# Reordering the first products of two accumulation stages in a cross-attention and expert kernel

## The chip, the cores and the metric

The kernel runs on one core of one Trainium2 chip. The metric is device microseconds of one execution; several executions are timed and their median is given. A separate profiled execution gives the trace, with its own time beside its span (from the first to the last instruction).

The engines are named as the profile names them: PE is the matrix engine and PEld its weight loads, DVE the vector engine, ACT the engine for activation functions, POOL the general one, SP the one whose queue issues most of the transfers. PE writes its products to banks of the accumulation memory (PSUM); the kernel uses eight banks of 128 x 512 fp32.

## What is computed

One transformer layer over 2048 tokens of width 256, in fp32: causal self attention, cross attention to 1601 context rows, a feed-forward block, and a layer of eight experts of which each token uses two.

```
def layer(y, Z):                       # y: layernorm of x, 4 blocks of 512 tokens here
    sa = attention(y, y, y, causal=True)
    y  = layernorm(y + sa, g1, beta1)
    ca = attention(y, Z, Z, causal=False)
    y  = layernorm(y + ca, g2, beta2)
    ff = relu(y @ w1 + b1) @ w2 + b2
    return layernorm(y + ff, g3, beta3)
x = x + layer(layernorm(x), ctx)
h = layernorm(x)
x = x + sum over the top 2 of 8 experts: weight * ((silu(h @ w1e) * (h @ w3e)) @ w2e)
```

In both attentions a score matrix is exponentiated without a division. The values carry a column of ones as a 257th column, so that one product gives the weighted sum and the sum of the weights together, and the division is made afterwards on 128 rows at a time.

## The kernel before

The 2048 tokens are four blocks (`b` = 0 to 3) of four tiles of 128 tokens (`j` = 0 to 3). The stages follow one another on PE: self attention of blocks 0, 1 and 2, the cross scores of block 0 (`cross_scores(0)`), self attention of block 3, and then for each block `cross_values(b)`, `cross_scores(b + 1)` and `ffn(b)`; last come the expert tiles. PE's order is the order in which the program is written (`manual_schedule` for the tensor engine, line 634). The other engines are put in order by a planner from the dependencies, except where the program says `issue_after`.

Eight banks are in three pools: `ps_s` with four (`bank_s`), `ps_o` with two (`bank_o`), `ps_t` with two. A pool hands out its banks in turn, and a bank is written again only when the last reader of its previous content is done. So the four accumulators of one stage take over the four `ps_s` banks that the stage before it used, in the same order.

Two stages matter here.

*Self attention of a block, `self_block` (lines 470 to 513).* `weigh` makes the scores of all 512 queries of the block against one tile of 128 keys in a `bank_o` (`scores`, line 380, products called `ss`), exponentiates them on ACT into a tile `pT` (line 363, four buffers), and masks the diagonal part on POOL (line 367). `values` (line 494, products called `acc`) multiplies the four query tiles with the values of these keys and adds into the four accumulators `acc[0..3]` of the block. The loop runs one step ahead: scores of step i + 1, then values of step i. The last step takes two key tiles together. When a query tile has seen its last key, `attended` (lines 388 to 393) empties its accumulator on DVE: a reciprocal (line 390), a scale and add to `h` (line 392, the last reader of the bank), and then the statistics and scaling of the layer norm (lines 227 to 250), with a power on POOL (line 233).

Block 0 has a routine of its own, `first_self`, which ends with `attended` for its four tiles. Block 1 is the first that goes through `self_block`; its four accumulators take the banks of block 0's.

*Cross values, `cross_values` (lines 599 to 628).* The exponentiated cross scores of a block lie in `raw`, 13 tiles of keys (12 of 128 and one of 65). For each tile of keys `k`, four products (line 604, called `co`), one per query tile `j`, add into the accumulators `co_0` to `co_3`. Then DVE empties these (lines 616 and 618), and the normalised rows are sent across partitions by transfers on SP's queue (`cross_over`, line 293, into `tb_y`) and turned by DVE (`turn_within`, line 305) into `yT`, which `ffn(b)` reads. These turns stand inside `cross_scores(b + 1)`, behind the maxima (line 561) of keys 6 and 8.

`cross_values(0)` stands right behind the self attention of block 3, so `co_0` to `co_3` take over the banks of that block's `acc_0` to `acc_3`. Between these two stages SP's queue also issues the crossing of block 3's rows (line 293), eight loads of expert weights `wo` (line 676) and two of `wi` (line 689, called at line 695).

Every fp32 product on PE is two records in the trace, so that the four products of one key tile are eight records.

Of the kernel before, what the change touches and what calls it, by code (L numbers as in the profile page):

```python
# [15 lines left out]
P = 128  # L16
# [3 lines left out]
def xattn_ffn_moe(  # L20
# [21 lines left out]
    nc = tc.nc  # L42

    S, D = x.shape
# [6 lines left out]
    TPB = TB // P  # L51
# [3 lines left out]
    NK = (SK + P - 1) // P  # L55
# [35 lines left out]
    def bank_s(name):  # L91
        return ps_s.tile([P, 512], F32, tag="s", name=name)

    def bank_o(name):
        return ps_o.tile([P, 512], F32, tag="o", name=name)
# [48 lines left out]
    z_sb = zpool.tile([P, NK, D + 1], F32, tag="z", name="z_sb")  # L144
# [94 lines left out]
    def normalize(dst, src, name, gain=None, shift=None, whole=None, behind=None):  # L239

        mean, rs = moments(src if whole is None else whole, name)
        if gain is None:
            return scaled(dst, src, mean, rs).ins
        n = work.tile([P, D], F32, tag="n", name=f"n_{name}")
        if len(dst.shape) > 2:
            n, gain, shift = qn(n), qn(gain), qn(shift)
            src = qn(src) if len(src.shape) == 2 else src
        nc.vector.scalar_tensor_tensor(n, src, mean, gain, ALU.subtract, ALU.mult)
        with tc.issue_after(behind) if behind is not None else ExitStack():
            return nc.vector.scalar_tensor_tensor(dst, n, rs, shift, ALU.mult, ALU.add).ins  # L250
# [22 lines left out]
    def quarters(b):  # L273


        together = ya[b].rearrange("p j n -> p (j n)")[:, : TPB * D]
        return together.rearrange("p (q j n) -> p q j n", q=NQ, j=TPB)

    def mid(t):
        return quarters(t // TPB)[:, :, t % TPB, :]  # L280

    def qn(a):
        return a.rearrange("p (q n) -> p q n", q=NQ)

    def crossing(name, b):
        return tbp.tile([P, TPB * D], F32, tag="tb", name=f"tb_{name}_{b}")

    def cross_over(tb, js, src):


        o, n = js[0], len(js)
        for q in range(NQ):
            last = nc.sync.dma_start(
                tb[q * Q : (q + 1) * Q, o * D : (o + n) * D], src[:, q, o : o + n, :]
            )
        return last.ins

    def turn_within(tb, into, js, behind=None, order="p i (c r) -> p i c r"):

        o, n = js[0], len(js)  # L300
        of = tb[:, o * D : (o + n) * D].rearrange("p (i j m) -> p i j m", i=NQ, j=n)
        for k, j in enumerate(js):
            to = into[:, :, j * P : (j + 1) * P]
            with tc.issue_after(behind) if behind is not None else ExitStack():
                done = nc.vector.transpose(
                    to.rearrange("p c (t i) -> p i c t", i=NQ),
                    of[:, :, k, :].rearrange(order, r=Q),
                )
        return done.ins
# [11 lines left out]
    for t in range(NT):  # L321
# [3 lines left out]
        else:  # L325
            b, j = divmod(t, TPB)
# [33 lines left out]
    def attend(pt, s):  # L360


        nc.scalar.activation(pt, s, AF.Exp, scale=SCALE)  # L363

    def mask(pt):

        nc.gpsimd.affine_select(
            pt,
            pt,
            pattern=[[1, P]],  # L370
            compare_op=ALU.is_ge,
            fill=0.0,
            base=0,
            channel_multiplier=-1,
        )

    def scores(s, b, kt, j0, j1):

        for c in range(ND):
            nc.tensor.matmul(  # L380
                s,
                lhsT=y0T[kt // TPB][:, c, (kt % TPB) * P : (kt % TPB + 1) * P],
                rhs=y0T[b][:, c, j0 * P : j1 * P],
                start=(c == 0),
                stop=(c == ND - 1),
            )

    def attended(acc, t):
        r = small.tile([P, 1], F32, tag="r", name=f"r1_{t}")
        nc.vector.reciprocal(r, acc[:, D : D + 1])  # L390
        h = work.tile([P, D], F32, tag="h", name=f"h1_{t}")
        nc.vector.scalar_tensor_tensor(h, acc[:, :D], r, y0[t][:, :D], ALU.mult, ALU.add)  # L392
        normalize(mid(t), h, f"1_{t}", g1b, be1b)
# [76 lines left out]
    def self_block(b, ptp, hooks):  # L470
        acc = [bank_s(f"acc_{b}_{j}") for j in range(TPB)]
        last = (b + 1) * TPB - 1

        def weigh(kts):

            s = bank_o(f"ss_{b}_{kts[0]}")
            pt = ptp.tile([P, TB], F32, tag="pt", name=f"pT_{b}_{kts[0]}")
            at, of = 0, []
            for kt in kts:

                j0 = max(0, kt - b * TPB)
                n = TB - j0 * P
                scores(s[:, at : at + n], b, kt, j0, TPB)
                of.append((kt, pt[:, at : at + n], j0))
                at += n
            attend(pt[:, :at], s[:, :at])
            for kt, p, _ in of:
                if kt >= b * TPB:
                    mask(p[:, :P])
            return of  # L490

        def values(kt, pt, j0):
            for j in range(j0, TPB):
                nc.tensor.matmul(  # L494
                    acc[j][:, : D + 1],
                    lhsT=pt[:, (j - j0) * P : (j - j0 + 1) * P],
                    rhs=y0[kt],
                    start=(kt == 0),
                    stop=(kt == b * TPB + j),
                )  # L500
            if kt >= b * TPB:
                attended(acc[j0], b * TPB + j0)


        steps = [[kt] for kt in range(last - 1)] + [[last - 1, last]]
        p = weigh(steps[0])
        for i in range(len(steps)):
            nxt = weigh(steps[i + 1]) if i + 1 < len(steps) else None
            for of in p:
                values(*of)  # L510
                if of[0] in hooks:
                    hooks[of[0]]()
            p = nxt
# [23 lines left out]
    raw = cp.tile([P, NK, TB], F32, tag="raw", name="raw")  # L537
# [5 lines left out]
    def keys(k):  # L543
        return P if k < KFULL else KREST
# [53 lines left out]

    def cross_values(b, js, hooks):
        acc = {j: bank_s(f"co_{b}_{j}") for j in js}  # L600
        for k in range(NK):
            n = keys(k)
            for j in js:
                nc.tensor.matmul(  # L604
                    acc[j][:, : D + 1],
                    lhsT=raw[:n, k, j * P : (j + 1) * P],
                    rhs=z_sb[:n, k, :],
                    start=(k == 0),
                    stop=(k == NK - 1),
                )  # L610
            if k in hooks:
                hooks[k]()
        for j in js:
            t = b * TPB + j
            r = small.tile([P, 1], F32, tag="r", name=f"r2_{t}")
            nc.vector.reciprocal(r, acc[j][:, D : D + 1])
            with tc.issue_after(turned_half[-1]) if turned_half else ExitStack():
                nc.vector.scalar_tensor_tensor(
                    mid(t), qn(acc[j][:, :D]), r, mid(t), ALU.mult, ALU.add
                )  # L620
        for j in js:
            t = b * TPB + j
            normed2.append(normalize(mid(t), mid(t), f"2_{t}", g2b, be2b))
        if b not in crossed:
            crossed[b] = crossing("y2", b)
        for h in range(0, len(js), 2):
            if b < LAST or js[0] == 0:
                cross_over(crossed[b], js[h : h + 2], quarters(b))


    ALL = range(TPB)
# [8 lines left out]
    for b in range(NB):  # L640
# [7 lines left out]
        hooks = {}  # L648
# [460 lines left out]
    def place_at(b):  # L1109
        puts = routed[b]()  # L1110
        if b == NB - 1:
            return puts
        for put in puts:
            put()
        if b == NB - 3:
            tabs["ex0"], tabs["row0"], tabs["done"] = tables_0()
        if b == NB - 2:
            tabs["exa"], tabs["rowa"], tabs["done"] = tables_a(tabs["done"])

    for b in range(NB - 1):  # L1120

        cross_values(b, ALL, {10: lambda: route_at(b - 1)} if b > 0 else {4: lambda: turn_y1(LAST)})
        hooks = {3: lambda: place_at(b - 1)} if b > 0 else {}
        cross_scores(b + 1, hooks, {6: ALL[:2], 8: ALL[2:]})
        ffn(b, ALL, {1: lambda: largest(b + 1), 3: lambda: exponentials(b + 1)})

    b, H = NB - 1, TPB // 2
    cross_values(b, ALL[:H], {})
    cross_values(b, ALL[H:], {NK - 1: lambda: turned_half.append(turn_within(crossed[b], yT[b], ALL[:H]))})
    load_xf(b)  # L1130
    route_at(b - 1)
# [153 lines left out]
    def turn_tile(n):  # L1285
        if n < len(tiles):
            xT[n] = turn_in(tiles[n][0], xs.pop(n))
# [11 lines left out]
    with tc.manual_schedule(engines={nc.sync.engine}):  # L1299
# [9 lines left out]
    hooks = {  # L1309
        2: lambda: turn_within(crossed[b], yT[b], ALL[H:]),  # L1310
        4: lambda: place_at(b - 1),
        NF - 1: lambda: [turn_tile(n) for n in range(2)],
    }
# [144 lines left out]
```

## Time and profile before

| what | us |
|---|---|
| three timed executions | 639.84, 642.43, 643.62 (median 642.43) |
| the profiled execution: its own time | 642.52 |
| the profiled execution: its span | 640.70 |
| PE busy in the span | 623.8 (97%) |
| PEld busy | 408.8 (64%) |
| DVE busy | 332.4 (52%) |
| POOL busy | 169.8 (26%) |
| ACT busy | 141.7 (22%) |

The stages of the profiled execution, by the start times of PE's instructions from the start of the span:

| stage | from, us | to, us |
|---|---|---|
| self attention of block 0 | 1.5 | 17.2 |
| self attention of blocks 1 and 2 | 17.2 | 77.6 |
| cross scores of block 0 | 77.6 | 99.9 |
| self attention of block 3 | 99.9 | 150.5 |
| cross values of block 0 | 150.5 | 174.7 |
| cross scores of block 1 | 174.7 | 197.0 |
| feed-forward of block 0 | 197.0 | 224.5 |
| blocks 1 and 2 in the same way | 224.5 | 373.8 |
| cross values and feed-forward of block 3 | 373.8 | 426.4 |
| expert tiles | 426.4 | 632.5 |
| last scatter and end | 632.5 | 640.7 |

A line of the timeline gives a start, a length, an engine and line, the operation with its output and inputs, and how many records were merged into it. In square brackets stands the idle time of the engine ahead of it and what ended it. The length of a matmul record reaches over the start of the next one, because products overlap in the array; the distance from one start to the next is the pace.

### The profile page before, as it was taken

The page shows a single profiled execution, that of the slowest core. Times are in us where ns is not written, and L with a number is a line of the kernel's source. Part 1 is how long each engine was busy: PE and PEld are TensorE (multiplying, and loading weights), DVE is VectorE, ACT ScalarE, POOL GpSimd, SP SyncE. Part 2 cuts the span into 40 slices and gives each one's busy share as a digit, 9 for nine tenths or more (in the row PEclk, how much of TensorE's full clock was granted, in tenths as well). Part 3 has the DMA queues.
Part 4 walks back from the last instruction along what each step waited for, and adds up shares of the span by engine and source line. Part 5 has one row for each costly group of instructions (what it writes and reads, how often), then busy time and mean ns, then how long its engine had stood idle before and what let it go on. Part 6 is the DMA issues. An engine that isn't in the chain of part 4 may idle for free. (4 is left out here: it accounts for less than half of the span.)

```text
span 640.7 us, 8263 instructions
## 1 busy us (share of the span) xinstructions
PE 623.8 (97%) x2255; PEld 408.8 (64%) x2256; DVE 332.4 (52%) x1011; ACT 141.7 (22%) x251; POOL 169.8 (26%) x240
## 2 busy tenths in 40 slices
PE   9999999999999999999999999999999999999993
PEld 8576745667845687467854688876665555555552
DVE  6662363504274476763587567737743344434341
ACT  3111132123033501352033600334211111111110
POOL 6221100002050032701155022443363222222222
PEclk9999999999999999999999999999999999999998
DMA  8999997001930012200312004953455555555532
GB/s 213 265 250 291 323 246 205 1 0 58 330 105 4 0 28 76 79 20 1 92 37 72 2 13 142 330 153 63 58 103 115 103 97 95 100 105 98 94 76 31
DMA packets 105549, 71.63 MB, mean 112 GB/s; under 512 B 43357, under 2 KB 99870, under 8 KB 105502
## 3 DMA queue, kind: packets, MB, share of 16 engines
q1 hardware_dynamic: 82510, 54.65, 31.9%
q0 software_dynamic: 6864, 9.08, 8.5%
q10 hardware_dynamic: 16128, 7.35, 4.0%
q8 instruction: 20, 0.33, 0.2%
q14 instruction: 27, 0.22, 0.1%
HBM read 28.11 MB, written 29.30 MB: 90 GB/s over the span
## 5 line engine op out<-in xcount | busy, mean ns | idle before, releaser
L233 POOL TENSOR_TENSOR rs<-ve,neghalf 128x1 f32<-128x1 f32 x80 | 47.6, 602 | 214.6 <-DVE ve L231 212.0
L604 PE MATMUL co<-z_sb,raw 128*128 128x257 f32 (+1 forms) x416 | 91.9, 381 | 1.1 <-DVE r L390 1.0
L551 PE MATMUL cs<-yT,zT_sb 128*128 128x512 f32 (+1 forms) x208 | 90.4, 593 | 0.0
L604 PEld LDWEIGHTS co<-z_sb,raw 128*128 128x128 f32 (+1 forms) x416 | 78.6, 190 | 13.0 <-issue 1.9
L551 PEld LDWEIGHTS cs<-yT,zT_sb 128*128 128x128 f32 (+1 forms) x208 | 38.5, 186 | 47.7 <-issue 46.1
L1207 PE MATMUL h_a<-wi,xT_a 128*128 x136 | 62.5, 594 | 0.0
L743 PE MATMUL fo<-w_sb,fhs 128*128 128x256 f32 x256 | 61.1, 380 | 0.0
L494 PE MATMUL acc<-y,pT 128*128 128x257 f32 x252 | 60.2, 381 | 0.8 <-DVE h L392 0.5
L721 PE MATMUL fh<-yT,w_sb 128*128 128x512 f32 (+1 forms) x160 | 60.9, 508 | 0.0
L494 PEld LDWEIGHTS acc<-y,pT 128*128 128x128 f32 x252 | 47.4, 190 | 18.8 <-issue 12.4
L743 PEld LDWEIGHTS fo<-w_sb,fhs 128*128 128x128 f32 x256 | 48.3, 190 | 16.0 <-issue 8.6
L558 ACT COPY raw<-cs 128x512 f32<-128x512 f32 (+1 forms) x52 | 30.4, 585 | 92.9 <-PE cs L551 92.9
L380 PE MATMUL ss<-y0T,y0T 128*128 128x512 f32 x96 | 44.6, 592 | 0.0
L1207 PE MATMUL h_b<-wi,xT_b 128*128 x96 | 43.3, 592 | 0.0
L730 ACT ACTIVATE fhs<-fh,b_sb 128x512 f32<-128x512 f32 (+1 forms) x40 | 24.0, 600 | 81.8 <-PE fh L721 81.8
L721 PEld LDWEIGHTS fh<-yT,w_sb 128*128 128x128 f32 x160 | 30.0, 190 | 17.2 <-issue 13.1
L1258 POOL DMA_INDIRECT out_dram<-yw_a,at_a x17 | 26.6, 1565 | 52.9 <-DVE yw_a L1256 29.4
L363 ACT ACTIVATE pT<-ss 128x512 f32<-128x512 f32 (+3 forms) x37 | 20.8, 562 | 86.8 <-PE ss L380 84.0
L561 DVE TENSOR_TENSOR top<-cs,top 128x512 f32<-128x512 f32 (+1 forms) x44 | 30.2, 687 | 16.9 <-ACT raw L558 16.0
L1207 PEld LDWEIGHTS h_a<-wi,xT_a 128*128 128x128 f32 x136 | 25.1, 190 | 21.8 <-issue 21.0
L1248 PE MATMUL y_a<-wo,gT_a 128*128 x136 | 32.4, 381 | 1.5 <-DVE gT_a L1231 1.5
L1248 PEld LDWEIGHTS y_a<-wo,gT_a 128*128 128x128 f32 x136 | 25.1, 190 | 13.6 <-DVE gT_a L1231 7.1
(267 smaller groups left out, 748.7 us busy)
## 6 DMA issues: line engine op xcount, KB each, us to landing
slots<-empty SPq DMA_DIRECT2D x8, 2064.0 KB
wo<-in_m2T_dram SPq DMA_DIRECT2D x8, 512.0 KB
wi<-in_m1T_dram SPq DMA_DIRECT2D x4, 1024.0 KB
wi<-in_m3T_dram SPq DMA_DIRECT2D x4, 1024.0 KB
gb_b<-g_b ACTq DMA_DIRECT2D x44, 64.0 KB
gb_a<-g_a ACTq DMA_DIRECT2D x36, 64.0 KB
xs_a<-slots SPq DMA_DIRECT2D x68, 32.0 KB
tb_y<-ya SPq DMA_DIRECT2D x16, 128.0 KB
```

What stands on the lines that cost most here:

```text
L233: raised.append(nc.gpsimd.tensor_tensor(rs, ve, neghalf, ALU.pow).ins)
L380: nc.tensor.matmul(s, lhsT=y0T[kt // TPB][:, c, (kt % TPB) * P : (kt % TPB + 1) * P], rhs=y0T[b][:, c, j0 * P : j1 * P], start=(c == 0), s ...
L494: nc.tensor.matmul(acc[j][:, : D + 1], lhsT=pt[:, (j - j0) * P : (j - j0 + 1) * P], rhs=y0[kt], start=(kt == 0), stop=(kt == b * TPB + j),)
L551: nc.tensor.matmul(s[:n, :], lhsT=zT_sb[:, c, k * P : k * P + n], rhs=yT[b][:, c, :], start=(c == 0), stop=(c == ND - 1),)
L558: acted.append(nc.scalar.copy(raw[:n, k, :], s[:n, :]).ins)
L561: topped = nc.vector.tensor_tensor(top[:n, :], s[:n, :], raw[:n, 0, :] if k == 1 else top[:n, :], ALU.max).ins
L604: nc.tensor.matmul(acc[j][:, : D + 1], lhsT=raw[:n, k, j * P : (j + 1) * P], rhs=z_sb[:n, k, :], start=(k == 0), stop=(k == NK - 1),)
L721: nc.tensor.matmul(s[:, :n], lhsT=w1_sb[:, c, f * P : (f + 1) * P], rhs=yT[b][:, c, q0 : q0 + n], start=(c == 0), stop=(c == ND - 1),)
L743: nc.tensor.matmul(acc[j], lhsT=h[:, i * P : (i + 1) * P], rhs=w2_sb[:, f, :], start=(f == 0 and i % 2 == 0), stop=(f == NF - 1), skip_gro ...
L1207: nc.tensor.matmul(into, lhsT=xT[:, c, :], rhs=wi[n, c].rearrange("p e i -> p (e i)")[:, bass.ds(w[0], I)], start=(c == 0), stop=(c == ND ...
L1248: nc.tensor.matmul(y[:, :D], lhsT=gT[:, i, :], rhs=wo[:, bass.ds(w[1] + i * D, D)], start=(i == 0), stop=(i == NI - 1),)
L1258: nc.gpsimd.indirect_dma_start(out=into, out_offset=bass.IndirectOffsetOnAxis(ap=at_token[:, 1:].bitcast(I32), axis=0), in_=yw, in_offset= ...
```

## The change

It changes the order of products on PE at two places and nothing else. No instruction is added or removed, and the order on DVE, ACT, POOL and SP is the same as before.

In `self_block`, for block 1 and its first step alone, `values` is split: `acc_0` and `acc_1` are done at their place, then come the scores of key tile 2 (`ss_2`), and only then `acc_2` and `acc_3` of the first step, ahead of the values of the second.

In `cross_values`, for block 0 alone, the twelve products of the first three key tiles are put in another order: `co_0` and `co_1` of keys 0, 1 and 2 in turn (six products), then `co_2` of keys 0, 1, 2, then `co_3` of keys 0, 1, 2. From key 3 on the order is as before.

```diff
-        def values(kt, pt, j0):
-            for j in range(j0, TPB):
+        def values(kt, pt, j0, js=ALL):
+            for j in js[j0:]:
                 nc.tensor.matmul(
                     acc[j][:, : D + 1],
                     lhsT=pt[:, (j - j0) * P : (j - j0 + 1) * P],
...
         steps = [[kt] for kt in range(last - 1)] + [[last - 1, last]]
-        p = weigh(steps[0])
+        p, late = weigh(steps[0]), None
         for i in range(len(steps)):
             nxt = weigh(steps[i + 1]) if i + 1 < len(steps) else None
+            if late:
+                values(*late, ALL[2:])
+
+            late = p[0] if b == 1 and i == 0 else None
             for of in p:
-                values(*of)
+                values(*of, ALL[:2] if late else ALL)
                 if of[0] in hooks:
                     hooks[of[0]]()
             p = nxt
...
     def cross_values(b, js, hooks):
         acc = {j: bank_s(f"co_{b}_{j}") for j in js}
-        for k in range(NK):
+        steps = [(k, j) for k in range(NK) for j in js]
+        if b == 0:
+            head = len(js) * 3
+            steps[:head] = sorted(steps[:head], key=lambda s: (s[1] > 1, s[0] if s[1] < 2 else s[1]))
+        for k, j in steps:
             n = keys(k)
-            for j in js:
-                nc.tensor.matmul(
...
-            if k in hooks:
+            nc.tensor.matmul(
+                acc[j][:, : D + 1],
+                lhsT=raw[:n, k, j * P : (j + 1) * P],
+                rhs=z_sb[:n, k, :],
+                start=(k == 0),
+                stop=(k == NK - 1),
+            )
+            if j == js[-1] and k in hooks:
                 hooks[k]()
```

## The prediction

> **What bounds the kernel now.** I read the page's table of engines first, then the list of what PE waits for over the whole span, and then the timeline of PE round the two places that the diff touches.
>
> ```profile
> PE 623.8 (97%) x2255; PEld 408.8 (64%) x2256; DVE 332.4 (52%) x1011; ACT 141.7 (22%) x251; POOL 169.8 (26%) x240
> ```
>
> PE is busy for 97% of the span, the next engine for 52% (PEld runs under PE). So a microsecond that PE stands still is a microsecond of the total, unless PE must wait for something on the clock later. What stops PE, from the list of waits for PE alone:
>
> ```profile
> engine line waited for: us in total, times, longest us
> PE y_b L1248 <- DVE gT_b L1231: 2.0, 2, 1.5
> PE warm L405 <- POOL ident masks.py:199: 1.5, 1, 1.5
> PE y_a L1248 <- DVE gT_a L1231: 1.5, 2, 0.8
> PE co L604 <- DVE r L390: 1.0, 1, 1.0
> ...
> PE acc L494 <- DVE h L392: 0.5, 1, 0.5
> ...
> PE co L604 <- DVE mv L229: 0.2, 1, 0.2
> ```
>
> Three of these rows lie where products are reordered: `acc` on `h` (block 1), and the two of `co`. Together 0.5 + 1.0 + 0.2 = 1.7 us. The other rows stand elsewhere and aren't touched. The PE timeline, first at the start of block 1, then at the start of the cross values:
>
> ```profile
> 20.66 1.46 PE L494 MATMUL acc<-y,pT 128*128 128x257 f32 x6
> 22.64 0.67 PE L494 MATMUL acc<-y,pT 128*128 128x257 f32 x2 [0.52 <-DVE h L392]
> 23.14 1.88 PE L380 MATMUL ss<-y0T,y0T 128*128 128x512 f32 x4
> 24.86 1.90 PE L494 MATMUL acc<-y,pT 128*128 128x257 f32 x8
> 26.60 0.59 PE L380 MATMUL ss<-y0T,y0T 128*128 128x512 f32 x1
> ```
> ```profile
> 150.51 1.03 PE L604 MATMUL co<-z_sb,raw 128*128 128x257 f32 x4
> 152.50 0.67 PE L604 MATMUL co<-z_sb,raw 128*128 128x257 f32 x2 [0.96 <-DVE r L390]
> 153.35 21.49 PE L604 MATMUL co<-z_sb,raw 128*128 128x257 f32 x98 [0.17 <-DVE mv L229]
> 174.68 1.88 PE L551 MATMUL cs<-yT,zT_sb 128*128 128x512 f32 x4
> ```
>
> In block 1, `acc_0`, `acc_1`, `acc_2` (six records) run, and `acc_3` stands. In the cross values `co_0`, `co_1` of key 0 run, `co_2` stands, and then `co_3`. What each stands for is on DVE:
>
> ```profile
> 22.01 0.48 DVE L392 SCALAR_TENSOR_TENSOR h<-acc,r,y 128x256 f32<-128x256 f32 x1
> ...
> 151.87 0.48 DVE L392 SCALAR_TENSOR_TENSOR h<-acc,r,y 128x256 f32<-128x256 f32 x1
> ...
> 152.73 0.47 DVE L392 SCALAR_TENSOR_TENSOR h<-acc,r,y 128x256 f32<-128x256 f32 x1
> ```
>
> These are the last readers of the old accumulators. They end at 22.49, 152.35 and 153.20, and PE goes on 0.15 us behind each (22.64, 152.50, 153.35): banks, not operands, are what is waited for. The label "r L390" on the long wait is only the neighbour that the profile picked.
>
> **What the change removes.** I take starts, not the idle column. Undisturbed, eight `acc` records take 26.60 - 24.86 = 1.74 us (0.217 each). From 20.66 to 23.14 they took 2.48, so this stall costs 0.74. An undisturbed stage of 104 `co` records, block 3's from 373.84 to 396.42, takes 22.58; block 0's took 174.68 - 150.51 = 24.17, so its two stalls cost 1.59. Sum **2.33 us**. The idle column gives 0.52 + 0.96 + 0.17 = 1.65 for the same places. I choose 2.33, since only starts say when the next product went in; 1.65 is the lower bound. The Trainium skill has a reason for the gap: "Perfetto Trace Analysis", section "Tensor Engine Instruction (MATMUL, LD_WEIGHTS)", says that a matmul's end is estimated from its size and not observed. By the idle column the time would be 640.8, by the starts 640.1; this trace agrees with that section, since 0.67 is shown for two records after the stall and 0.60 for two elsewhere.
>
> **What it puts in the way instead.** Both orders have the same products, so the adds are nothing but places; each is checked against who must be ready.
>
> Block 1: `acc_0`, `acc_1` from 20.66 (4 x 0.217 = 0.87), then `ss_2` from 21.53 for 1.72 (24.86 - 23.14), then `acc_2`, `acc_3` from 23.25 and 23.68. The bank of `acc_3` is free at 22.64: 1.0 us to spare. `ss_2` comes 1.6 us earlier than now; its bank was `ss_0`'s, which ACT finished reading at 19.81 (an exponential of 0.60 from 19.21), 1.7 us before. The held-back products keep the first `pT` busy until 24.1; the fourth exponential after it, which takes that buffer, comes at 32.02. Values of step 1 then start at 24.12, with their exponential done at 21.52. Next in line are the transposes of block 2 at 33.50, whose rows DVE has finished at 29.55: 3.9 us to spare against a shift of 0.74.
>
> Until the cross values the 0.74 is kept, for all that feeds PE there is fed by PE. One wait stays: 0.26 at 149.10 for a mask on POOL. It follows a chain of ACT without a gap from the score exponential at 141.57, which itself waits for PE, so it moves along and keeps its length.
>
> Cross values: in the old clock, six products take 150.51 to 153.11; `co_2` wants its bank at 153.11 and has it at 152.50 (0.6 to spare), `co_3` at 154.41, has it at 153.35 (1.1). The `raw` tiles of keys 1 and 2 are exponentiated by 144.76 (five of them in 2.69 from 142.07), 6 us ahead. Without that cover the wait returns as before, at most 1.59.
>
> Three products in a row now add into one bank. No `co` row shows that. The nearest: `cs`, two products per bank, 0.43 per record of 512 columns; and `y` (line 1248), four per bank, 1.73 for eight records of 256. Both keep the pace of 0.217 per 256 columns, so the price is 0; the upper bound, products that don't overlap at all (0.381 a record, the mean in the page), would be 4 products x 2 records x 0.164 = 1.3 us.
>
> What is late next: DVE, and so SP, is not sped up by 1.59, only by 0.74. SP issues the weights `wo` and `wi` behind block 3's rows, from 156.44; the transfer engines are full until 179.2, in the change until 178.5. The crossing of block 0's rows is issued at 179.56, just behind that; in the change at 177.23, so 1.2 us of it meets full engines. Its first half lands by about 184 and its second by about 187.6 (transfer rates in slices of 0.4 us); DVE turns them at 188.17 and 191.61, with no idle time ahead. Spare time of 4 us covers 1.2, price 0.
>
> Nothing behind 197 is tied to a clock: each transfer is issued after a PE product of its own stage. So the sum stands: the span 640.70 becomes 638.37; with the 1.82 us around it 640.19 against the profiled 642.52, and **640.1 us** against the median of 642.43 (-0.36%).
>
> **The rivals.**
>
> *One place only.* If one stall comes back at its new place (a bank still late, or the three-in-a-row at 1.3), the gain is 0.74 to 1.59: 640.8 to 641.7. For it: the spare 0.6 us at `co_2` is small. Against: it is fixed by DVE's order, which doesn't change. 9%.
>
> *It does nothing*, the gain being eaten by a later wait: 642.4. PE waits 0.5 to 1.5 us at six places among the experts, but each behind transfers that PE's own products start. 5%.
>
> *More than that.* A short idle could slow PE's pace after it. The trace has a slow pace at the very start: 16 warming records of 128 columns take 5.17 - 1.52 = 3.65, 0.228 each, where the four from 33.50 take 0.115 each; that is 1.8 lost (the granted clock reads 1.00 there too, so pace is the better witness). The same behind each of the two places would add 3.6 to the gain: 636.5. Against: the `co` records behind the stall run 98 in 174.68 - 153.35 = 21.33, 0.2177 each, against 0.2171 in block 3, at most 0.06 us in all. The Trainium skill, "TensorE: Matmul & The Clock Gate", section "A second HAM failure mode: psum-queue depth-cycling", tells of losses from such micro-idles; the trace shows none behind these. 2%.
>
> *Slower.* The crossing of block 0 gets stuck behind the weights. Four transfers of that kind issued under full engines took 9.58 us (SP from 48.09) where the four from 156.44 took 3.27: 6.3 late, twice 12.6 if both halves suffer. It decides from the point where DVE's second turn makes `yT` late for the feed-forward: 4.0 us of spare in landing, and 196.99 - 192.7 = 4.3 from the end of the turn to that stage, 8.3 in all. Beyond it PE loses 12.6 - 8.3 = 4.3, net of 2.33 gained 2.0 slower than before: 644.4. Against: the engines are full for 1.2 us of it, not for 12. 7%.
>
> **How the numbers follow.** The forecast has the remaining 77%. Half a per cent is 3.2 us, about what a measurement of this kernel tells from no change; the gain is 2.3, so faster by that much needs 639.2 or less. The three runs shown lie 3.8 apart, so a median can be off by 1 or 2: I give 25 of the 77 to below 639.2 and 52 to within. Faster: 25 and the 2 of the pace, 0.27. Slower by so much is 645.7 or more, 1.3 above the slow rival's time: 3 of its 7 by scatter, 0.03. Within: 52 + 9 + 5 + 4, 0.70. The range reaches from 638.0 (forecast less 2.1, the scatter) to 642.8 (no gain, with some scatter).
>
> **What would show it.** In the changed kernel's PE timeline no idle time ahead of `acc` near 23 us and of `co` near 150; from the first `acc` of block 1 to the first of the next step 3.46 us, not 4.20; 22.6 us from the first `co` to the first `cs`, not 24.2; the stages behind 197 of the same length. Wrong: a wait of `co_2`, `cs` or the first `fh` of line 721 in their place, or a longer crossing of block 0 on SP.

## The result and the profile after

Over 18 runs of each, the kernel before took 641.92 us (median, 639.65 to 643.77) and the changed one 639.35 (637.76 to 640.99): ratio 0.996, 95% interval 0.995 to 0.9971. That is 2.57 us less, where 2.33 was forecast; with the interval, 1.9 to 3.2. The three runs shown before the prediction had a median half a microsecond above that of the 18, which is why 639.35 lies under the forecast 640.1 although the gain came out nearly as reckoned.

The profiled execution of the changed kernel took 640.99, with a span of 639.3. The page's table of engines, and from the list of waits those of PE (line numbers behind the edit are 4 to 9 higher than before):

```profile
PE 624.5 (98%) x2255; PEld 409.5 (64%) x2256; DVE 332.5 (52%) x1011; ACT 141.8 (22%) x251; POOL 169.6 (27%) x240
```
```profile
PE y_b L1257 <- DVE gT_b L1240: 1.7, 2, 1.5
PE warm L405 <- POOL ident masks.py:199: 1.5, 1, 1.5
PE y_a L1257 <- DVE gT_a L1240: 1.0, 2, 0.6
...
PE acc L494 <- POOL pT L367: 0.3, 1, 0.3
```

The rows of `co` on DVE and of `acc` on `h` are gone; the wait of `acc` on the mask stands as it was. The only row that is new is one of 0.2 at 7.42 us, in the starting phase ahead of both places. The PE timeline at the two places (start, length, engine, line, operation, records):

```profile
20.69 1.03 PE L494 MATMUL acc<-y,pT 128*128 128x257 f32 x4
21.56 1.88 PE L380 MATMUL ss<-y0T,y0T 128*128 128x512 f32 x4
23.28 2.76 PE L494 MATMUL acc<-y,pT 128*128 128x257 f32 x12
25.88 1.45 PE L380 MATMUL ss<-y0T,y0T 128*128 128x512 f32 x3
```
```profile
148.38 1.57 PE L494 MATMUL acc<-y,pT 128*128 128x257 f32 x6 [0.26 <-POOL pT L367]
149.79 22.72 PE L613 MATMUL co<-z_sb,raw 128*128 128x257 f32 x104
172.35 4.03 PE L555 MATMUL cs<-yT,zT_sb 128*128 128x512 f32 x9
```

Two accumulators, the scores, and then twelve records without a break: `acc_2` and `acc_3` of the first step and the eight of the next. These eight start at 23.28 + 4 x 0.217 = 24.15, 3.46 us behind the first `acc`, as forecast, where it was 4.20. The 104 `co` records are one unbroken group of 172.35 - 149.79 = 22.56 us; it was 24.17. No wait stands in their place: DVE works as before, and PE does other products until the last banks are free. The last readers of these banks in the changed kernel:

```profile
151.16 0.48 DVE L392 SCALAR_TENSOR_TENSOR h<-acc,r,y 128x256 f32<-128x256 f32 x1
...
152.01 0.47 DVE L392 SCALAR_TENSOR_TENSOR h<-acc,r,y 128x256 f32<-128x256 f32 x1
```

They end at 151.64 and 152.48. PE reaches `co_2` six products behind 149.79, at 152.39, and `co_3` at 153.69: 0.6 and 1.1 us to spare behind PE's usual 0.15, the numbers of the prediction. (The profile does not name banks; these spares are reckoned, and the unbroken group agrees with them.)

Everything from 172.35 to the router's transposes is earlier by 2.33 us (`cs` 174.68 to 172.35, `pt_xn` 441.87 to 439.54). Yet the spans of the two profiled executions differ by 1.4 only. The missing 0.9 went behind 443. The stretches there, one per line, with the granted clock third from the end:

```profile
443.00:444.00 1.00, 1.00 (x2) 0.34 (x1) 0.62 (x4) 0.88 (x2) 0.00 (x0) 0.53 0.81 105
444.00:445.00 1.00, 1.00 (x2) 0.23 (x1) 0.84 (x5) 0.63 (x1) 0.00 (x0) 0.50 0.76 105
445.00:446.00 1.00, 1.00 (x6) 0.99 (x5) 0.90 (x7) 0.60 (x1) 0.16 (x1) 0.50 0.54 76
446.00:447.00 1.00, 1.00 (x3) 0.39 (x2) 0.62 (x6) 0.58 (x1) 1.00 (x1) 0.76 0.27 39
```

For 3.4 us PE ran at half clock: 0.47 + 0.50 + 0.50 + 0.24 = 1.7 us lost. The profiled execution of before did not have this; its stretch over the same work, which comes 2.3 us later there, reads 1.00 throughout:

```profile
442.00:452.00 10.00, 9.81 (x45) 6.32 (x46) 6.36 (x29) 4.61 (x8) 3.20 (x2) 1.00 0.56 83
```

The waits that follow gave back the rest of the difference (from 0.78 to 0.38 at the first of them). The timed runs show that this differs from execution to execution: the changed kernel's runs with a mean clock (the granted clock over the whole span, 1 being full speed) of 0.993 took 640.4 to 641.0, those at 0.996 and 0.997 took 637.8 to 638.7. One profiled execution per kernel is thus no measure of a change of 2 us, but its stages are.

### The profile page after: what moved, and what is told of

It is laid out like the page before. It is cut to its first block, busy times and chain, and to the rows that moved or that the text cites. A ratio compares the mean times of both kernels' runs of the same rounds, so it can differ in the third digit from the quotient of the medians.

```text
span 639.3 us, 8263 instructions
## 1 busy us (share of the span) xinstructions
PE 624.5 (98%) x2255; PEld 409.5 (64%) x2256; DVE 332.5 (52%) x1011; ACT 141.8 (22%) x251; POOL 169.6 (27%) x240
## 5 line engine op out<-in xcount | busy, mean ns | idle before, releaser
L1216 PE MATMUL h_a<-wi,xT_a 128*128 x136 | 63.8, 604 | 0.0
```

What stands on the lines that cost most here:

```text
L1216: nc.tensor.matmul(into, lhsT=xT[:, c, :], rhs=wi[n, c].rearrange("p e i -> p (e i)")[:, bass.ds(w[0], I)], start=(c == 0), stop=(c == ND ...
```

## The experiments

The theory: each place gave back its own stall, measured from start to start (0.74 and 1.59), and nothing else changed. The rivals: one place alone does it, the order is faster in itself, or a later wait takes it back. The half-clock spell was a second question: is it brought on by what PE does there? The experiments ran on the chips numbered 9, 2 and 12, each beside the kernel before; it took 645.4 to 646.4 there, 3.5 to 4.4 us more than above, and the end of the document shows where most of this lies.

**Block 1 alone.**

```diff
-        if b == 0:
+        if False:
             head = len(js) * 3
```

> Block 1's first step is reordered as in the change, the cross values are left in the old order. My theory (each place gives back its own stall, by starts): block 1's first eight acc records and ss_2 lose 0.74 us, so first acc to first acc of the next step is 3.46 us and not 4.20; the stretch from the first co to the first cs stays 24.17 us with its idle times of 0.96 and 0.17; the total is 0.74 us under before, ratio 0.999. Rival (the gain comes from one place alone, the other is eaten later): the start of the cross values is not 0.7 earlier than 150.5, ratio 1.000. By the idle column the gain would be 0.52.

Block 1 was as in the changed kernel (first `acc` 20.68, `ss_2` 21.55, twelve records from 23.27). The cross values kept their stalls:

```profile
149.78 1.03 PE L613 MATMUL co<-z_sb,raw 128*128 128x257 f32 x4
151.78 0.67 PE L613 MATMUL co<-z_sb,raw 128*128 128x257 f32 x2 [0.97 <-DVE r L390]
152.63 21.49 PE L613 MATMUL co<-z_sb,raw 128*128 128x257 f32 x98 [0.17 <-DVE mv L229]
173.96 3.60 PE L555 MATMUL cs<-yT,zT_sb 128*128 128x512 f32 x8
```

The first `co` is at 149.78 and not 150.51: the 0.73 gained in block 1 arrives in full, 128 us later. The stage then takes 24.18 as before. In this one profile PE stood again at 349.78, 0.61 us for ACT in the feed-forward of block 2, and the cross values of block 3 began no earlier than before (374.00 against 373.84). No other profile has this wait, those with the same order in block 1 included, and nothing tried here explains it. The total says less: 646.44 against 646.35, ratio 1.0, interval 0.9975 to 1.0024, which holds both 0.999 and 1.000; that the 0.73 reaches the end is shown by no total of its own.

**The cross values alone.**

```diff
-            late = p[0] if b == 1 and i == 0 else None
+            late = None
```

> The cross values are reordered as in the change, block 1 is left as before. My theory: 0.52 us of idle time stays near 22.6 us; first co to first cs takes 22.6 us and not 24.17; everything behind it is 1.59 us earlier; ratio 0.9975. Rival (the later weight and crossing transfers eat it): cs or the first fh waits, ratio 1.000. By the idle column the gain would be 1.13.

The idle time in block 1 stayed, 0.53 ahead of 22.67. The `co` group ran unbroken from 150.54 to `cs` at 173.10, 22.56 us, 1.61 less than before. `cs` and `fh` had no wait (`fh` at 195.42, 22.32 behind the first `cs`, as in the kernel before). Ratio 0.998, interval 0.9961 to 1.0. The two parts add up to the whole: 0.73 + 1.61 = 2.34.

**The same order where there is no stall.**

```diff
-            late = p[0] if b == 1 and i == 0 else None
+            late = p[0] if b > 0 and i == 0 else None
...
-        if b == 0:
+        if b < LAST:
             head = len(js) * 3
```

> The same reorderings at all blocks: block 1, 2 and 3's first step and the cross values of blocks 0, 1 and 2. Only block 1 and block 0 had a wait for a bank there. My theory (the order is worth only the wait that it covers): no stage gets shorter than in the changed kernel, the cross values of blocks 1 and 2 keep the pace of 0.217 a record; ratio to before 0.996 as in the change. Rival (grouped products or an earlier score are faster or slower in themselves): the stages of blocks 1, 2 and 3 change by about the same amounts as block 1 and block 0 did, 0.7 and 1.6 each, so a total off by 2 us or more.

No stage moved. In block 2 the first scores to the scores of the fifth key tile take 52.56 - 40.50 = 12.06 us, against 52.71 - 40.64 = 12.07 in the changed kernel; the first 88 `co` records of block 1 take 19.10 against 19.09. The total is 0.9979 of before, 0.9957 to 1.0001, which tells neither from the change nor from no gain; the stages decide. So here an order that covers no wait is worth nothing, and three products in a row into one bank cost nothing: the pace is 0.217 a record either way.

**Two key tiles instead of three.**

```diff
-            head = len(js) * 3
+            head = len(js) * 2
```

> The changed kernel, with two key tiles instead of three reordered in the cross values of block 0. Theory (banks): co_2 wants its bank four products after the first co, 149.79 + 4 x 0.434 = 151.53; DVE's h ends 1.85 behind the first co and PE goes on 0.15 later, 151.79: co_2 starts 0.26 late, idle time shown about 0.1 (0.26 less the 0.16 by which a product's drawn length exceeds the pace), then nothing at co_3; first co to first cs 22.9 us, against 22.6 with three keys and 24.2 with none. Rival (what counts is that products of one bank stand together, or an operand): 22.6, or still over 23.5.

```profile
149.80 23.05 PE L613 MATMUL co<-z_sb,raw 128*128 128x257 f32 x104
172.69 4.89 PE L555 MATMUL cs<-yT,zT_sb 128*128 128x512 f32 x11
```

22.89 us: 0.33 more than with three tiles, where 0.3 was expected, so the third tile is needed and the cover counts as reckoned. No idle time is drawn on PE at all. In the records of the trace, the ninth of the group starts 0.26 late and the one behind it another 0.08; the modelled length of a record (0.38) reaches 0.16 past the pace, so that 0.09 of idle time is left, the 0.1 that was expected, and the timeline and the list of waits leave out one so short. Only the weight loads show it, as 0.5 of "issue". A stall of a third of a microsecond can thus be absent from the list of waits. A single execution was timed of this version and of the next (647.99 and 641.75), so their totals say nothing.

**The order the wrong way round.**

```diff
-            steps[:head] = sorted(steps[:head], key=lambda s: (s[1] > 1, s[0] if s[1] < 2 else s[1]))
+            steps[:head] = sorted(steps[:head], key=lambda s: (s[1] < 2, s[0] if s[1] < 2 else s[1]))
```

> The changed kernel with the first three key tiles of block 0's cross values the wrong way round: the six products of co_2 and co_3 first, then co_0 and co_1. Theory (banks): the first co stands until acc_2's bank is free, which is 2.0 us behind the point where the first co starts in the changed kernel (149.8; DVE's h for that row ends at 151.64, PE 0.15 later): idle time shown about 1.8 (2.0 less the 0.16 by which a product's drawn length exceeds the pace), once; co_3 comes 1.3 later and finds its bank free (152.64). From the end of the acc products' pace at 149.8 to the first cs 24.6 us, 2.0 to 2.1 more than in the change. Rival (the order of banks doesn't matter): 22.6.

This expectation failed: the 104 records ran unbroken from 149.76 to 172.32, 22.56 us, as in the change, although DVE read the old accumulators at the same times (the last two `h` end at 151.61 and 152.46). `co_2` cannot have stood in the bank of `acc_2` then, so the expectation was wrong that the names fix the banks. The reading that fits is that a bank goes to an accumulator when that one is first written, so that whichever comes first gets the bank that is free first; the profile names no banks, so this is inferred from this one run. The change's gain then does not hang on the names `co_0` and `co_1`; it is that only two accumulators are opened early. The run exposes no stall and so does not test the bank theory against its rival; the block 1 run, where the third accumulator is opened at once and stands, and the run with two key tiles do.

**The router's transposes spread.**

In the changed kernel the half-clock spell follows a stretch in which PE makes little:

```profile
438.69 0.60 PE L256 MATMUL pt_xn<-ident,ya 128*128 128x128 f32 x4
439.54 0.71 PE L256 MATMUL pt_xn<-ident,ya 128*128 128x128 f32 x4 [0.24 <-ACT yT L257]
440.44 1.95 PE L834 MATMUL lp<-wg_sb,yT 128*128 128x8 f32 x16 [0.18 <-ACT yT L257]
442.25 2.97 PE L1216 MATMUL h_a<-wi,xT_a 128*128 x4
445.01 1.06 PE L1249 MATMUL gtp_a<-ident,g_a 128*128 128x128 f32 x4
```

Eight transposes (one record each), two waits and the sixteen records of eight products of 8 columns fill 438.69 to 442.25; the four `h_a` records behind them take 2.76 us. In the kernel before they took 1.80:

```profile
444.58 1.96 PE L1207 MATMUL h_a<-wi,xT_a 128*128 x4
446.38 0.60 PE L1240 MATMUL gtp_a<-ident,g_a 128*128 128x128 f32 x4
```

The next version takes the transposes apart and leaves the 8-column products together.

```diff
+                if n == LATE:
+                    turn_last(0)
+                    turn_last(1)
                 hidden(name, xT[n], w, 0, h1)
...
                 hidden(name, xT.pop(n), w, 1, h3)
+                if n == LATE:
+                    turn_last(2)
...
         if b == LAST:
-            for j in range(TPB):
-                t = b * TPB + j
-                of = [row(t)[:, c * P : (c + 1) * P] for c in range(ND)]
-                transpose_to(turned(t), of, f"xn_{t}", nc.scalar.copy)
+            turn_last(TPB - 1)
```

> The changed kernel, with the four transposes of the last block's rows (line 256, pt_xn) taken apart: two ahead of expert tile 2's first products, one behind its second products, one at the old place ahead of the router products lp. In the profile of the changed kernel PE ran at half clock for 3.4 us from 443.5, right behind a stretch of 3.6 us (438.7 to 442.3) in which it made only these transposes, waited 0.24 and 0.18, and made products of 8 columns. Theory A (thin work on PE is followed by a spell at half clock, in some executions): the thin stretch is 1.8 us instead of 3.6, no granted clock under 1.00 behind it, the mean clock of the runs lies at 0.995 or above, and the median is 0.5 to 1.5 us under the changed kernel's 639.35. Theory B (the spell has nothing to do with what PE does there): clocks of 0.993 and 0.994 in about half of the runs as before, and only the two waits are saved, some 0.6 us by starts.

The thin stretch was still 442.53 to 445.26, 2.7 us, and the spell came again (four `h_a` from 445.26 took 3.0); the mean clocks of 12 runs were 0.991 to 0.997, median 0.993, and the kernel before beside it had the same median. Ratio to before 0.998, 0.9959 to 1.0001. This tells nothing between A and B: 1.8 us of thin work was the aim, 2.7 was made.

**The changed kernel again, and the router's products spread too.** Three versions were run side by side: the changed kernel; one that takes the router's `lp` products apart as well as the transposes; and one that adds to this a new order for the last step of each self attention (the last lines of the diff).

```diff
                 hidden(name, xT[n], w, 0, h1)
+                if n == LATE:
+                    lp_last[:] = [bank_s(f"lp_{LAST}")]
+                    logits(LAST, (0, 1))
+                if n == LATE + 1:
+                    route_at(NB - 1)
...
         if n == LATE:
-            route_at(NB - 1)
+            logits(LAST, (2,))
+            turn_last(3)
...
-            for j in js[j0:]:
+            for j in js[j0:] if kt < last - 1 else js[j0:][::-1]:
```

The changed kernel:

> The changed kernel once more, as the yardstick on this chip for the two versions beside it. My theory: ratio to before 0.996 (2.3 us); first co to first cs 22.6 us, no idle time near 23 and 150. If the gain hung on the chip's state, 1.000.

With nothing thin:

> The changed kernel with the transposes pt_xn and the router products lp of the last block spread out: two transposes ahead of expert tile 2's first products, the lp products of two tiles behind them, one transpose behind the second products, lp of the third tile and the last transpose at the old place, the last lp behind the next tile's first products. No thin stretch on PE is longer than 0.7 us where it was 3.6 (and 2.7 in the run with the transposes alone spread, where a half-clock spell still followed). Theory A (thin work brings the spell): no granted clock under 1.00 between 430 and 460, the runs' mean clocks 0.002 to 0.003 above those of the changed kernel beside it, and 1.0 to 2.0 us less than it (0.4 of that from the two waits). Theory B (the spell is independent of PE's work): the same clocks as the changed kernel, at most 0.6 us less.

And with the last step turned round:

> As the version with nothing thin, and in the last step of each self attention the products whose scores are masked on POOL come last (acc_3 ahead of acc_2 for the last key tile but one). My theory: the wait of 0.26 for pT on POOL at 148.4 goes, 0.42 us by starts; block 1 and 2's last steps, which had no such wait, keep their length; the total is 0.4 us under the version with nothing thin. Rival: the wait only moves to acc_2 or to acc_3's second product, no gain.

| kernel, 12 runs each | median us (lowest to highest) | to before, 95% | mean clocks |
|---|---|---|---|
| changed | 643.17 (640.74 to 645.25) | 0.9976 (0.9957 to 0.9995) | 0.991 to 0.996 |
| and nothing thin | 641.74 (640.68 to 643.53) | 0.9953 (0.9936 to 0.997) | 0.995 to 0.998 |
| and last step turned | 641.72 (639.41 to 644.35) | 0.996 (0.9941 to 0.9978) | 0.994 to 0.998 |

The kernel before took 645.37 beside them, with clocks of 0.990 to 0.998. By the medians the change gains 2.2 us here again; its ratio, which is not the quotient of the medians, gives 1.5, with 0.3 to 2.8. With nothing thin, no run falls under a clock of 0.995, and the median is 1.43 us under the changed kernel's, inside the 1.0 to 2.0 of theory A. (The longest thin stretch left is 1.0 us, 443.10 to 444.14, not 0.7.) Its profile has no clock under 1.00 in the stretches from 440 to 460:

```profile
440.00:445.00 5.00, 4.74 (x22) 3.16 (x21) 3.33 (x10) 0.96 (x3) 1.70 (x4) 1.00 0.47 131
445.00:450.00 5.00, 5.00 (x22) 3.31 (x21) 1.99 (x7) 3.22 (x5) 1.93 (x2) 1.00 0.55 77
```

The profile of the changed kernel beside it had a spell (0.66 from 445 to 450). So thin work on PE brings the spell on; this rests on the clocks and on the window count at the end more than on the totals.

In the third, the wait of 0.26 on the mask is gone:

```profile
146.75 2.87 PE L494 MATMUL acc<-y,pT 128*128 128x257 f32 x12
149.46 22.72 PE L613 MATMUL co<-z_sb,raw 128*128 128x257 f32 x104
```

From the first of these `acc` to the first `co` it is 2.71 us, against 149.82 - 146.69 = 3.13 in the version without it: the 0.42 forecast; the last steps of blocks 1 and 2 keep their length (2.60 us in block 2 in both). The totals are the same within their scatter (641.72 and 641.74), so 0.4 us is shown by the stage alone. Both versions are faster than the kernel before, with intervals wholly below 1; over the changed kernel the advantage is 0.2%, which the intervals to before do not separate.

## Why the prediction was right

- *Bank waits, to be read from starts.* Right. The stages shrank by 0.73 and 1.61 in separate runs and by 2.33 together, as 0.74, 1.59 and 2.33 were reckoned; the idle column's 1.65 was too little, by some 0.23 a stall. A record is drawn 0.38 long at a pace of 0.217, which hides 0.16; and the second record behind a stall starts 0.29 behind the first instead of 0.217. The prediction's 0.67 against 0.60 is this second part, and does not show by itself that ends are estimated.
- *The cover is enough.* Right, with the spare 0.6 and 1.1 us as worked out; two key tiles were too few by the 0.3 that the same arithmetic gave.
- *Three products in a row into one bank cost nothing.* Right: 22.56 us for 104 records.
- *The mask's wait stays, 0.26.* Right (148.38).
- *The crossing of block 0 meets the weights for 1.2 us and is hidden.* Right: SP issued it from 177.24, its eight issues took 7.08 us as before, DVE's turns came at 185.85 and 189.28 without idle time, 2.3 earlier each.
- *Nothing behind 197 hangs on a clock.* Right for what PE waits for; what the sum left out is PE's own clock, which in that one execution took back 1.7 us behind the router. The waits on `gT` among the experts are not bound to PE alone either: the first four summed to 2.6 us before and 2.0 in that execution, where PE came later. The spell does not look like a consequence of the change: in the runs beside the last group the kernel before had clocks of 0.990 to 0.998 and the changed one 0.991 to 0.996, with a median of 0.994 for both.
- *Slower pace behind short idles, given 2%.* It is not found at the two places that were changed, as argued from the pace. A slow clock behind little work exists, at another place and behind a longer thin stretch; the window count at the end says why the stalls did not bring it on.

The measured 2.57 is 0.24 more than the sum; the interval (1.9 to 3.2) does not tell the two apart. That the forecast of 640.1 came out 0.75 too high is mostly the median of three runs that it started from, and not the mechanism.

## What to carry to other kernels

Where accumulators of a new stage wait for an old stage's banks to be emptied, open only as many as have free banks, and go deeper into the sum with these; the number of steps needed follows from the time at which the last reader ends. Take the price of a stall on PE from starts against an undisturbed stage, not from the idle column: here 2.33 against 1.65. Small products that stand together on PE for some 3 us can cost more than their own time: interleave them with full ones.

## What was not expected of the hardware

PE's clock halves behind thin work even where PE is drawn as busy. Behind 2.7 to 3.6 us of transposes and 8-column products, with waits of 0.2 between them, the clock stood at half for 3.4 us in some executions and not in others; the same sixteen `lp` records inside the cross values, 1.7 us between full products, never showed it in these profiles. The Trainium skill, "TensorE: Matmul & The Clock Gate", section "What's actually happening", tells of a window of 3413 ns that is free-running, with half rate after an idle one. The length agrees with the stretches above (0.53, 0.50, 0.50, 0.76 of four microseconds), and a window whose phase differs from run to run would explain why only some executions have it.

The clock records of the kept traces bear this out. In each of the eleven traces every change of the clock lies a whole number of windows of 3.413 us behind the point at which its clock record begins: in the changed kernel the clock is full for 128 such windows, half for one (443.06 to 446.48) and full for 55. This grid lies differently against the program from execution to execution: the record begins 4.9 to 7.0 us into the span. For each window I estimate how much of it PE's products fill, from their starts and columns at the full pace seen here (512 columns in 0.43 us). Of the 1957 windows at full clock that begin between 10 and 620 us, six are filled to 0.22 to 0.37, and each of these is followed by one window at half clock; all others are filled to 0.43 or more, and none of them is. So the windows ahead of a spell were not idle: at most 0.37 of work was little enough here. (Behind 620 us, where PE runs out of work, one window of 0.37 was not followed by one.) Five of the six hold the router's work, the sixth a stall of 2.81 us in the run with two key tiles. Where the same router's work had no spell, it was cut otherwise by the grid: its emptiest window was filled to 0.43 in the kernel before, to 0.43, 0.44 and 0.51 in three experiments, and to 0.73 and 0.75 in the two versions with nothing thin. The window with the stalls of the cross values was filled to 0.52 in the kernel before, above that line. These traces place the line between 0.37 and 0.43 by this estimate, for this kernel's products only.

In the experiments PE also stood 2.2 to 3.0 us, in one piece or two, in the feed-forward of block 3, where the first profiles of before and after have nothing. The PE timeline of the run with the cross values alone, and its stretches before and during it (transfer share last but one):

```profile
421.16 1.13 PE L752 MATMUL fo<-w_sb,fhs 128*128 128x256 f32 x4 [2.96 <-issue]
```
```profile
412.00:416.00 4.00, 4.00 (x20) 3.38 (x19) 2.20 (x13) 1.42 (x3) 3.08 (x4) 1.00 1.02 366
416.00:420.00 4.00, 2.20 (x11) 1.59 (x9) 0.00 (x0) 0.00 (x0) 3.08 (x4) 1.00 1.10 376
```

ACT made nothing from 415.4 to 420.6 (5.27 us, put down to "issue") and PE stopped behind it, while transfers kept their engines full. Full transfer engines alone do not bring it on: in the first profile of the changed kernel they were as full (1.03 and 0.96 in the same two stretches), and PE did not stop. What ACT waited for is not in the profile, and was not tried. The stall stands in all nine profiles of the experiments. From the first `co` of block 3 to the first `h_a` they take 55.4 to 55.8 us (57.3 in the run with two key tiles, which has a half-clock spell behind the stall) where the first profiles of before and after take 52.55: some 3 us of the 3.5 to 4.4 by which their times lie higher.
